# Later first flags of `adj`, far terms a block ahead of the masks, and another order of the last pair's products and rows in a two-layer graph kernel

## The chip, the cores and the metric

The kernel runs on one core of a Trainium2 chip. The metric is device time in microseconds (us), and lower is better. Three runs of the kernel before took 1580.74, 1581.55 and 1582.32 us; the median is 1581.55 us.

The core has five engines that run side by side, each with its own instructions in a fixed order: TensorE (PE in the profile), VectorE (DVE), ScalarE (ACT), GpSimd (POOL) and SyncE (SP). SP and POOL issue nearly all transfers here. The profile's clock of TensorE is given as a share of its full speed.

## The reference

`x` is 4096 x 512, `adj` 4096 x 4096 with some 0.8% of ones. Cut to what matters:

```python
# layer 0
keep = (adj > 0) & (cumsum(adj > 0, axis=1) <= 64)
cnt  = keep.sum(axis=1)
xj = leaky_relu(((keep @ x) / max(cnt, 1)) @ W_nb.T + b_nb)
xi = leaky_relu(x @ W_line.T + b_line)
x  = layernorm(x + xi + where(cnt > 0, xj, 0))
# layer 1
Wh = x @ W + bW
e  = (Wh @ a1 + b1)[:, None] + (Wh @ a2 + b2)[None, :]
e  = where(adj > 0, where(e > 0, e, 0.2 * e), -9e15)
x  = layernorm(x + softmax(e, axis=1) @ Wh)
```

## The kernel before, in words

The rows are 32 blocks of 128. The work runs in four stages, with times from the trace of the profiled execution.

**Linear parts of layer 0 (0 to 218 us).** TensorE computes `x @ W_nb.T` and `x @ W_line.T` first, so that `adj` later multiplies finished rows. After the first two blocks this goes by pairs of blocks, `seven(g, last, codes)` for g = 1 to 13 (the last only ends the pair before): seven products of half-size blocks in place of eight (Strassen's scheme in Winograd's form). Each `product` is two matmuls (four records in the trace, two for each). In the order of TensorE, pair g does: `x_g` with `w11`; the third product of the pair before, `x_p` with `t3`; `bank_z` with `t1`; the pair before's `bank_w` with `w22`; `x_g` with `t2`; the pair before's `x_p` with `t4`; `bank_y` with `w21`. Between them ScalarE copies and bends results, and VectorE transposes the next two blocks of `x` (`turn_pair`, line 325), adds, and forms the low half `y_lo` (line 418) of what ScalarE rounded to `y_hi` (line 417). Line 548 copies `x_g` into `bank_y` and so must wait until line 418 has read the old `bank_y`. `turn_pair` also issues the load of the block three on, `load_turned_x`: four transfers on POOL's queue, line 298.

Into four gaps of each `seven` go steps of another task, the argument `codes`, which finds for each row of `adj` the first 64 ones. Half a row block (2048 columns) at a time is loaded (`load_adj`, SP's queue, line 164), turned into flags by ScalarE (`edge`, line 175), counted by a running sum on VectorE (`scan_sums`, `scan_codes`), packed into bytes by ScalarE (`pack`, line 223) and written out. There are two buffers of each kind, so a load waits for the `edge` two before. At g = 1 the steps are instead `fold_w` (line 386), ten VectorE multiplications that fold `W` with `a1` and `a2`, the small write `wa_d` by SP (line 393), and `edge(0)`. Until the last `fold_w` the rows `a1` and `a2` lie in the buffer that `edge(0)` writes.

**Neighbour sums of layer 0 (218 to 682 us).** Line 741, bound by TensorE; the change doesn't touch it.

**`Wh` of layer 1 (682 to 795 us).** A loop of 32 steps s: four matmuls of block s (line 1045), then VectorE adds the bias for the step before (`finish_wh`, line 818) and transposes the block for step s + 3 (`turn_x1`, line 809). From step 8 on, the weights of the first two blocks of layer 1 are computed beside it. For each quarter block i: `mask` is a ScalarE activation that gives 0 or a huge number, the far term (line 855), and a VectorE subtraction that also takes the row's maximum (line 858); `score` bends the result on ScalarE (line 847). With four quarters done, `greatest` joins the four maxima on VectorE, `shift` bends them (four tiny ScalarE operations, line 847) and forms the negative shift on VectorE (line 891), and `weigh` takes the exponential on ScalarE (line 900), beside the next block's masks.

**Products with the weights (795 us to the end).** 16 pairs of blocks; each sums seven products (`consume`, line 959) over four parts into four PSUM tiles of two halves each, in the order of the table `order`. For the last pair the order is 4, 1, 2, 6, 7, 5, 3, so 4 and 1 share a tile, 2 and 6, 7 and 5, and 3 has its own. The code from line 1109 on ends the last pair. It joins the products into the rows `top` and `low`, scales, adds the residual, normalizes and writes; the `low` row comes first, the `top` row last, in two halves.

The order on each engine is the order of the code (no scheduler moves it); tiles and semaphores only add waits. The lines to follow are these:

```python
601                elif g > 1:
602                    steps = [
603                        lambda: (load_adj(q + 2), edge(q + 1)),
942    order = {True: (1, 2, 4, 7, 5, 6, 3), False: (4, 1, 2, 6, 7, 5, 3)}
```

Of the kernel before, what the change touches and what calls it, by code (L numbers as in the profile page):

```python
# [9 lines left out]
F32 = mybir.dt.float32  # L10
# [22 lines left out]
def two_layer_adj_gnn(  # L33
# [103 lines left out]
    with ExitStack() as l0:  # L137
# [33 lines left out]
        def edge(s):  # L171
            if s < NB * NCH:
                b, h = divmod(s, NCH)
                edge_of[s] = halves_of(adj_p.tile([P, CH], BF16, name="edge"))
                nc.scalar.activation(  # L175
                    edge_of[s], loaded.pop(s).rearrange("p (t q) -> p q t", q=2),
                    AF.Sigmoid, bias=steep[:, 0:1], scale=STEEP,
                    accum_out=cnts[:, h, b : b + 1],
                )
# [103 lines left out]
        with ExitStack() as la:  # L283
# [99 lines left out]
            def fold_w(c):  # L383
                wn = raw["w"][c] if c < NC else early_rows[2]
                for k in range(2):
                    nc.vector.scalar_tensor_tensor(  # L386
                        early_rows[3], wn, 1.0, early_rows[k], ALU.mult, ALU.mult,
                        accum_out=wa[:, k, c : c + 1] if c < NC else ca[:, k : k + 1],
                    )
# [49 lines left out]
            turn_x(1)  # L439
            load_turned_x(4)  # L440

            first = [pls[0]]

# [58 lines left out]
            line(0)  # L502
            bend(0)
            pls[1] = linear(xts.pop(1), "line")
            first.append(pls[1])
            x_top[0] = xt_tile()
            y_low = y_terms(1, pys[1])
            sums_x(1)
# [10 lines left out]

            bank_y, bank_z = pys.pop(0), first[0]
            bank_x, bank_w = [pys.pop(1)], first[1]
            bank_x += [ps_acc.tile([P, C], F32, name="acc") for _ in range(2)]
            low_row, low_line = {}, {}

# [64 lines left out]
            for g in range(1, EDGE // 2):  # L591
                steps = idle
                q = done[0]
                if g == 1:
                    steps = [
                        lambda: (load_adj(1), fold_w(0)),
                        lambda: (fold_w(1), fold_w(2)),
                        idle[0],
                        lambda: (fold_w(3), fold_w(NC), fold_end(), edge(0)),
                    ]  # L600
                elif g > 1:
                    steps = [
                        lambda: (load_adj(q + 2), edge(q + 1)),
                        lambda: scan_sums(q),
                        lambda: pack(q - 1),
                        lambda: scan_codes(q),
                    ]
                    done[0] += 1
                seven(g, False, steps)
# [188 lines left out]
                )  # L798

    x1ts, x1rows, pws, nats, wts, parts = {}, {}, {}, {}, {}, {}  # L800
    m4s, mms, nms, z4s, zqs, rzs, banks, sums = {}, {}, {}, {}, {}, {}, {}, {}

    FIRST = 8

# [41 lines left out]
        bias, scale = st_n[:, i, 0, b : b + 1], st_n[:, i, 2, b : b + 1]  # L846
        nc.scalar.activation(dst, src, AF.Prelu, bias=bias, scale=scale, alpha=0.2)  # L847

    def mask(b, i):

        if i == 0:
            wts[b] = early if b == 0 else wp.tile([P, NI, NS * SQ], F32, name="w")
            m4s[b] = stat.tile([P, NI], F32, name="m4", bufs=2)
        w_i = wts[b][:, i, :]
        nc.scalar.activation(  # L855
            w_i, nats[b, i // 2].bitcast(U8)[:, i % 2, :], AF.Relu, bias=far, scale=-FAR
        )
        nc.vector.tensor_tensor_reduce(  # L858
            w_i, e2_n, w_i, 1.0, -3e38, ALU.subtract, ALU.max, m4s[b][:, i : i + 1]
        )  # L860
        if i % 2:
            load_nat(b + 1, i // 2)

    def score(b, i):
        w_i = wts[b][:, i, :]
        bend1(b, i, w_i, w_i)
# [16 lines left out]
    def shift(b):  # L883


        mm = mms.pop(b)
        lm = stat.tile([P, NI], F32, name="lm", bufs=2)
        for i in range(NI):
            bend1(b, i, lm[:, i : i + 1], mm[:, i : i + 1])
        nms[b] = stat.tile([P, NI], F32, name="nm", bufs=2)  # L890
        nc.vector.scalar_tensor_tensor(  # L891
            nms[b], lm, -1.0, st_n[:, :, 1, b], ALU.mult, ALU.subtract
        )

    def weigh(b, i):
# [43 lines left out]
        }  # L939


    order = {True: (1, 2, 4, 7, 5, 6, 3), False: (4, 1, 2, 6, 7, 5, 3)}
    where = {key: {n: divmod(i, 2) for i, n in enumerate(o)} for key, o in order.items()}

    def consume(q):
# [95 lines left out]
    for s in range(NS):  # L1041
        pws[s] = ps_acc.tile([P, C], F32, name="acc")
        x1t = x1ts.pop(s)
        for m in range(NC):
            nc.tensor.matmul(  # L1045
                pws[s], x1t[:, m, :], ws[:, m, :], start=(m == 0), stop=(m == NC - 1)
            )
        if s > 0:
            finish_wh(s - 1)
        turn_x1(s + 3)  # L1050
        load_turned(s + 7)
        if s == 0:
            load_nat(0, 0)
            load_nat(0, 1)
        if FIRST <= s < FIRST + 8:
            b, i = divmod(s - FIRST, NI)
            mask(b, i)
            score(b, i)
        if FIRST + 4 <= s < FIRST + 12:
            b, i = divmod(s - FIRST - 4, NI)  # L1060
            if i == 0:
                greatest(b)
                shift(b)
            weigh(b, i)
        if s in range(FIRST + 14, FIRST + 22, 2):
            q, part = divmod((s - FIRST - 14) // 2, 2)
            (turn, combine)[part](q)
        elif s >= FIRST + 8:
            combine_wh()
    finish_wh(NS - 1)  # L1070

    for q in range(NP * NT):
        g, k = divmod(q, NP)
        consume(q)
        more = 0 < q < NP * NT - 1
        if more:
            turn(q + 1)

        b = {2: 2 * g + 3, 3: 2 * g + 4}.get(k, 2 if q == 0 else NB)
        if k == 3 and more:  # L1080
            combine(q + 1)
        if b < NB:
            for i in range(NI):
                mask(b, i)
# [26 lines left out]
    x_top, x_low = x1rows[NB - 2].rearrange("p (h c) -> p h c", h=2), x1rows[NB - 1]  # L1111
    stt = nc.vector.scalar_tensor_tensor
    st = stat.tile([P, 2, nc.vector.BN_STATS_DIM], F32, name="st2", bufs=1)
    nc.scalar.copy(top[:, 0], p[1])
    tt(top[:, 1], top[:, 0], p[6], ALU.add)
    tt(top[:, 0], top[:, 0], p[2], ALU.add)
    tt(low[:, 0], top[:, 1], p[7], ALU.add)
    stt(top[:, 0], top[:, 0], rz[:, 0:1], x_top[:, 0], ALU.mult, ALU.add)
    nc.vector.bn_stats(st[:, 0], top[:, 0])
    tt(low[:, 1], low[:, 0], p[5], ALU.add)  # L1120
    tt(low[:, 0], low[:, 0], p[4], ALU.subtract)
    y_low = low.rearrange("p h c -> p (h c)")
    stt(y_low, y_low, rz[:, 1:2], x_low, ALU.mult, ALU.add)
    low_stats = ln_stats(y_low)
    tt(top[:, 1], top[:, 1], p[5], ALU.add)
    stt(top[:, 1], top[:, 1], rz[:, 0:1], x_top[:, 1], ALU.mult, ALU.add)
    stt(top[:, 1], p[3], rz[:, 0:1], top[:, 1], ALU.mult, ALU.add)
    nc.vector.bn_stats(st[:, 1], top[:, 1])
    mv, rs = ln_rs(st)
# [39 lines left out]
```

## Time and profile before

| | |
|---|---|
| median of three runs | 1581.55 us |
| the profiled execution, its own time | 1579.91 us |
| its span in the trace | 1578.1 us |
| mean granted TensorE clock | 0.997 |
| TensorE busy | 1558.7 us (99%) |
| VectorE busy | 1257.6 us (80%) |
| ScalarE busy | 953.7 us (60%) |
| GpSimd busy | 240.6 us (15%) |

The span is the profiled execution from its first to its last instruction. Busy is the time in which an engine has an instruction running. In a timeline each line is a start, a length, the engine, the line of the kernel, the operation, what it writes and reads, and in brackets how long the engine stood idle before it and what ended that. The ends of matmuls are modelled, so distances between starts say more than lengths.

### The profile page before, as it was taken

To read this page: it belongs to the slowest core of one execution; us is meant where nothing else is said; L and a number is where in the kernel's file an instruction comes from. 1 tells how busy PE (TensorE), PEld (TensorE's weight loads), DVE (VectorE), ACT (ScalarE), POOL (GpSimd) and SP (SyncE) were. 2 spreads that over 40 slices of the span, in tenths; PEclk is the share of its full clock that TensorE was granted. 3 is DMA by queue.
4 is the path that set the end of the run, shared out by engine and by line. 5 is a ranking of instruction groups with operands and counts; after the bars stand their busy time and mean duration, and the time that the engine had idled before them with its cause. 6 is when DMAs were issued, how large, how long until landed. Compare 5 with 4: busy or idle time off the path is not lost.

```text
span 1578.1 us, 18600 instructions
## 1 busy us (share of the span) xinstructions
PE 1558.7 (99%) x6408; PEld 1209.3 (77%) x6408; DVE 1257.6 (80%) x2304; ACT 953.7 (60%) x1123; POOL 240.6 (15%) x397
## 2 busy tenths in 40 slices
PE   8999999999999999999999999999999999999997
PEld 4444468888888888854488888888888888888886
DVE  5888658999999998456998888788878878888863
ACT  3666558887888877416165675555765557755520
POOL 4454212222222122120000000000000000000000
PEclk9999999999999999999999999999999999999999
DMA  8756469889889987653211111111111111111100
GB/s 233 200 191 211 159 168 263 261 247 265 238 257 222 275 219 225 154 116 101 58 41 41 28 54 53 42 50 25 48 54 41 54 40 29 54 49 46 41 7 34
DMA packets 170430, 193.01 MB, mean 122 GB/s; under 512 B 101424, under 2 KB 134480, under 8 KB 162144
## 3 DMA queue, kind: packets, MB, share of 16 engines
q1 hardware_dynamic: 147968, 131.38, 30.3%
q0 software_dynamic: 21792, 59.53, 13.0%
q8 instruction: 50, 0.82, 0.2%
q10 hardware_dynamic: 576, 0.92, 0.2%
q14 instruction: 44, 0.36, 0.1%
HBM read 132.91 MB, written 42.08 MB: 111 GB/s over the span
## 4 chain that ended last, share of the span: by engine, by line
PE 95%; DMA 2%; DVE 2%; ACT 1%; issue 1%; SPq 0%; POOL 0%; POOLq 0%; DVEq 0%; ACTq 0%
PE acc L959 35%; PE acc L741 29%; PE pt L959 14%; PE acc L489 8%; PE acc L1045 5%; PE acc L371 2%; DMA a<-in_L_gnn_W_line_dram 1%; DMA c<-in_x_dram 1%; PE pt L371 0%; DMA w<-x_d 0%; DVE edge L386 0%; ACT w L855 0%; DMA own_d<-t 0%; DVE c L809 0%; POOL c L298 0%
## 5 line engine op out<-in xcount | busy, mean ns | idle before, releaser
L959 PE MATMUL acc<-bt,s 128*128 128x256 f32 x1536 | 342.6, 379 | 0.0
L959 PEld LDWEIGHTS acc<-bt,s 128*128 128x128 f32 x1536 | 291.8, 190 | 39.7
L741 PE MATMUL acc<-y_hi,kt 128*128 128x512 f32 x824 | 320.5, 389 | 0.0
L741 PE MATMUL acc<-y_lo,kt 128*128 128x512 f32 x824 | 320.5, 389 | 0.0
L855 ACT ACTIVATE w<-nat,few 128x1024 f32<-128x1024 uint8 x128 | 136.9, 1135 | 289.6 <-DVE a L919 238.9
L959 PE MATMUL acc<-bt,a 128*128 128x256 f32 x1024 | 232.1, 379 | 0.0
L959 PE MATMUL pt<-bt,a 128*128 128x256 f32 x1024 | 231.5, 379 | 0.0
L959 PEld LDWEIGHTS pt<-bt,a 128*128 128x128 f32 x1024 | 194.6, 190 | 26.9 <-issue 0.5
L959 PEld LDWEIGHTS acc<-bt,a 128*128 128x128 f32 x1024 | 194.6, 190 | 26.5
L277 ACT ACTIVATE kt<-ktb,few 128x1024 fp32r<-128x1024 uint8 x124 | 142.7, 1151 | 97.8 <-PE acc L741 80.1
L919 DVE STREAM_TRANSPOSE a<-w 128x1024 f32<-128x1024 f32 x128 | 153.0, 1224 | 57.8 <-ACT w L900 53.2
L126 POOL TENSOR_TENSOR rs<-ve,few 128x1 f32<-128x1 f32 x64 | 46.7, 730 | 945.8 <-DVE ve L124 933.1
L741 PEld LDWEIGHTS acc<-y_hi,kt 128*128 128x128 f32 x824 | 154.7, 188 | 32.2
L741 PEld LDWEIGHTS acc<-y_lo,kt 128*128 128x128 f32 x824 | 154.6, 188 | 32.1
L847 ACT ACTIVATE w<-w,st_n 128x1024 f32<-128x1024 f32 x128 | 149.4, 1233 | 39.0 <-DVE m L858 39.0
L858 DVE CUSTOM_DVE_ANT_0 w<-e_n,w 128x1024 f32<-128x1024 f32 x128 | 149.5, 1220 | 9.1 <-ACT w L855 7.7
L900 ACT ACTIVATE w<-w,nm 128x1024 f32<-128x1024 f32 x128 | 145.4, 1137 | 11.3 <-DVE nm L891 11.3
L175 ACT ACTIVATE edge<-a,few 128x2048 bf16<-128x2048 int32 x64 | 136.2, 2129 | 11.8 <-DVE edge L386 6.8
L223 ACT CAST code<-left 128x2048 uint8<-128x2048 bf16 x64 | 121.1, 1892 | 0.0
L1045 PE MATMUL acc<-w,c 128*128 128x512 f32 x232 | 100.3, 593 | 2.6 <-DVE c L809 2.6
L1045 PEld LDWEIGHTS acc<-w,c 128*128 128x128 f32 x232 | 43.9, 190 | 58.8 <-issue 52.1
L206 DVE TENSOR_TENSOR left<-edge,left 128x2048 bf16<-128x2048 bf16 x64 | 78.4, 1225 | 2.2
(187 smaller groups left out, 1885.3 us busy)
## 6 DMA issues: line engine op xcount, KB each, us to landing
a<-in_adj_dram SPq DMA_DIRECT2D x64, 1024.0 KB, 6.1
code_d<-code POOLq DMA_DIRECT2D x64, 256.0 KB, 4.0
nat<-code_d SPq DMA_DIRECT2D x256, 64.0 KB, 2.0
w<-x_d SPq DMA_DIRECT2D x128, 64.0 KB, 2.1
c<-in_x_dram POOLq DMA_DIRECT2D x124, 64.0 KB, 5.2
own<-in_x_dram SPq DMA_DIRECT2D x31, 256.0 KB, 3.3
own<-own_d POOLq DMA_DIRECT2D x31, 256.0 KB, 5.1
x_d<-own POOLq DMA_DIRECT2D x31, 256.0 KB, 4.7
```

What stands on the lines that cost most here:

```text
L175: nc.scalar.activation(edge_of[s], loaded.pop(s).rearrange("p (t q) -> p q t", q=2), AF.Sigmoid, bias=steep[:, 0:1], scale=STEEP, accum_ou ...
L223: nc.scalar.copy(code.bitcast(U8).rearrange("p (t q) -> p q t", q=2), seen_of.pop(s))
L277: nc.scalar.activation(kts[s], bytes_.rearrange("p t (i r) -> p t r i", r=2), AF.Sigmoid, bias=steep[:, 1:2], scale=STEEP,)
L489: nc.tensor.matmul(bank, lhs[:, k, :], rhs[:, k, :], start=start and k == 0, stop=k == 1, skip_group_check=True,)
L741: nc.tensor.matmul(accs[i], kt[:, k // 2, k % 2, :], term[j], start=(j == 0 and term is y_hi), stop=(j == NB - 1 and term is y_lo),)
L847: nc.scalar.activation(dst, src, AF.Prelu, bias=bias, scale=scale, alpha=0.2)
L855: nc.scalar.activation(w_i, nats[b, i // 2].bitcast(U8)[:, i % 2, :], AF.Relu, bias=far, scale=-FAR)
L858: nc.vector.tensor_tensor_reduce(w_i, e2_n, w_i, 1.0, -3e38, ALU.subtract, ALU.max, m4s[b][:, i : i + 1])
L900: nc.scalar.activation(w_i, w_i, AF.Exp, bias=nms[b][:, i : i + 1], accum_out=z4s[g][:, r, i : i + 1])
L919: nc.vector.transpose(a[:, r].rearrange("p s (i a) -> p i s a", a=SQ), wts[2 * g + r][:, :, ts(k, 8 * SQ)].rearrange("p i (s x) -> p i s x ...
L959: nc.tensor.matmul(banks[g][n], lhs[:, j, :], bt[:, 4 * k + j, rhs, :], start=(k == 0 and j == 0 and n == mate[0]), stop=(k == NP - 1 and ...
L1045: nc.tensor.matmul(pws[s], x1t[:, m, :], ws[:, m, :], start=(m == 0), stop=(m == NC - 1))
```

## The change

It has three parts. First, `edge(0)` moves from the end of pair 1 to the first gap of pair 2, and `edge(1)` from the first gap of pair 2 to its third gap, together with `load_adj(2)`. From pair 3 on the order is as before. Second, `mask` is split into `cover` (the ScalarE activation, and the load of the next bytes of `adj`) and `mask` (the VectorE subtraction); in the `Wh` stage `cover` runs one step ahead of its `mask`. `shift` is split into `bend_greatest` and `less`, and `greatest` moves to the end of the step before, so that two VectorE operations of the loop stand between the maxima and `less`. Third, for the last pair alone, the order of the products becomes 4, 1, 2, 6, 5, 3, 7, so that 5 and 3 share a tile and 7 has its own; the end of the kernel is written anew, with the `top` row whole and first, and the seventh product added to two halves of the `low` row. The name `first` becomes `wide` in one place, which moves nothing.

```diff
-                        lambda: (fold_w(3), fold_w(NC), fold_end(), edge(0)),
+                        lambda: (fold_w(3), fold_w(NC), fold_end()),
                     ]
-                elif g > 1:
+                else:
+                    first = [lambda: edge(0), lambda: (load_adj(q + 2), edge(q + 1))]
                     steps = [
-                        lambda: (load_adj(q + 2), edge(q + 1)),
+                        first[g > 2],
                         lambda: scan_sums(q),
-                        lambda: pack(q - 1),
+                        (lambda: pack(q - 1)) if g > 2 else first[1],
                         lambda: scan_codes(q),
                     ]
...
+    def cover(b, i):
+        if i == 0:
+            wts[b] = early if b == 0 else wp.tile([P, NI, NS * SQ], F32, name="w")
+            m4s[b] = stat.tile([P, NI], F32, name="m4", bufs=2)
+        nc.scalar.activation(
+            wts[b][:, i, :], nats[b, i // 2].bitcast(U8)[:, i % 2, :],
+            AF.Relu, bias=far, scale=-FAR,
+        )
+        if i % 2:
+            load_nat(b + 1, i // 2)
+
     def mask(b, i):
         w_i = wts[b][:, i, :]
-        nc.scalar.activation(
-            w_i, nats[b, i // 2].bitcast(U8)[:, i % 2, :], AF.Relu, bias=far, scale=-FAR
-        )
         nc.vector.tensor_tensor_reduce(
             w_i, e2_n, w_i, 1.0, -3e38, ALU.subtract, ALU.max, m4s[b][:, i : i + 1]
         )
-        if i % 2:
-            load_nat(b + 1, i // 2)
...
-    order = {True: (1, 2, 4, 7, 5, 6, 3), False: (4, 1, 2, 6, 7, 5, 3)}
+    order = {True: (1, 2, 4, 7, 5, 6, 3), False: (4, 1, 2, 6, 5, 3, 7)}
...
-        if FIRST <= s < FIRST + 8:
-            b, i = divmod(s - FIRST, NI)
-            mask(b, i)
-            score(b, i)
-        if FIRST + 4 <= s < FIRST + 12:
-            b, i = divmod(s - FIRST - 4, NI)
-            if i == 0:
-                greatest(b)
-                shift(b)
-            weigh(b, i)
+        k = s - FIRST
+        if k in (4, 8):
+            less(k // NI - 1)
+        if 0 <= k < 8:
+            mask(*divmod(k, NI))
+        if -1 <= k < 7:
+            cover(*divmod(k + 1, NI))
+        if 0 <= k < 8:
+            score(*divmod(k, NI))
+        if k in (3, 7):
+            greatest(k // NI)
+            bend_greatest(k // NI)
+        if 4 <= k < 12:
+            weigh(*divmod(k - 4, NI))
...
+    x_low = x_low.rearrange("p (h c) -> p h c", h=2)
     nc.scalar.copy(top[:, 0], p[1])
+    tt(low[:, 0], top[:, 0], p[4], ALU.subtract)
     tt(top[:, 1], top[:, 0], p[6], ALU.add)
     tt(top[:, 0], top[:, 0], p[2], ALU.add)
-    tt(low[:, 0], top[:, 1], p[7], ALU.add)
+    tt(low[:, 0], low[:, 0], p[6], ALU.add)
+    stt(low[:, 0], low[:, 0], rz[:, 1:2], x_low[:, 0], ALU.mult, ALU.add)
     stt(top[:, 0], top[:, 0], rz[:, 0:1], x_top[:, 0], ALU.mult, ALU.add)
     nc.vector.bn_stats(st[:, 0], top[:, 0])
-    tt(low[:, 1], low[:, 0], p[5], ALU.add)
-    tt(low[:, 0], low[:, 0], p[4], ALU.subtract)
-    y_low = low.rearrange("p h c -> p (h c)")
-    stt(y_low, y_low, rz[:, 1:2], x_low, ALU.mult, ALU.add)
-    low_stats = ln_stats(y_low)
     tt(top[:, 1], top[:, 1], p[5], ALU.add)
+    stt(low[:, 1], top[:, 1], rz[:, 1:2], x_low[:, 1], ALU.mult, ALU.add)
+    tt(top[:, 1], top[:, 1], p[3], ALU.add)
     stt(top[:, 1], top[:, 1], rz[:, 0:1], x_top[:, 1], ALU.mult, ALU.add)
-    stt(top[:, 1], p[3], rz[:, 0:1], top[:, 1], ALU.mult, ALU.add)
     nc.vector.bn_stats(st[:, 1], top[:, 1])
-    mv, rs = ln_rs(st)
-    ln_apply(y_low, low_stats)
-    nc.scalar.dma_start(out_blk(NB - 1), y_low)
+    top_stats = ln_rs(st)
     for h in range(2):
-        ln_apply(top[:, h], (mv, rs))
-        (nc.sync, nc.scalar)[h].dma_start(out_blk(NB - 2)[:, ts(h, HC)], top[:, h])
+        stt(low[:, h], p[7], rz[:, 1:2], low[:, h], ALU.mult, ALU.add)
+    low_stats = ln_stats(low.rearrange("p h c -> p (h c)"))
+    ln_apply(top.rearrange("p h c -> p (h c)"), top_stats)
+    nc.scalar.dma_start(out_blk(NB - 2), top.rearrange("p h c -> p (h c)"))
+    for h in range(2):
+        ln_apply(low[:, h], low_stats)
+        (nc.sync, nc.scalar)[h].dma_start(out_blk(NB - 1)[:, ts(h, HC)], low[:, h])
```

More of the change, by code (lines that the diff above doesn't have):

```diff
@@ L440, in two_layer_adj_gnn @@
             load_turned_x(4)
-            first = [pls[0]]
+            wide = [pls[0]]
             room_hi = last.tile([P, ONE_BY_ONE, C], F32, name="hi")
@@ L504, in two_layer_adj_gnn @@
             pls[1] = linear(xts.pop(1), "line")
-            first.append(pls[1])
+            wide.append(pls[1])
             x_top[0] = xt_tile()
@@ L517, in two_layer_adj_gnn @@
             own(1)
-            bank_y, bank_z = pys.pop(0), first[0]
-            bank_x, bank_w = [pys.pop(1)], first[1]
+            bank_y, bank_z = pys.pop(0), wide[0]
+            bank_x, bank_w = [pys.pop(1)], wide[1]
             bank_x += [ps_acc.tile([P, C], F32, name="acc") for _ in range(2)]
@@ L800, in two_layer_adj_gnn @@
     x1ts, x1rows, pws, nats, wts, parts = {}, {}, {}, {}, {}, {}
-    m4s, mms, nms, z4s, zqs, rzs, banks, sums = {}, {}, {}, {}, {}, {}, {}, {}
+    m4s, mms, lms, nms, z4s, zqs, rzs, banks, sums = ({} for _ in range(9))
     FIRST = 8
@@ L847, in bend1 @@
         nc.scalar.activation(dst, src, AF.Prelu, bias=bias, scale=scale, alpha=0.2)
-    def mask(b, i):
+    def cover(b, i):
         if i == 0:
@@ L853, in mask @@
             m4s[b] = stat.tile([P, NI], F32, name="m4", bufs=2)
+        nc.scalar.activation(
[4 more added lines that the diff above has]
+            load_nat(b + 1, i // 2)
+    def mask(b, i):
         w_i = wts[b][:, i, :]
-        nc.scalar.activation(
-            w_i, nats[b, i // 2].bitcast(U8)[:, i % 2, :], AF.Relu, bias=far, scale=-FAR
-        )
         nc.vector.tensor_tensor_reduce(
@@ L883, in shift, with bend_greatest, less @@
     def shift(b):
+        bend_greatest(b)
+        less(b)
+    def bend_greatest(b):
         mm = mms.pop(b)
-        lm = stat.tile([P, NI], F32, name="lm", bufs=2)
+        lms[b] = stat.tile([P, NI], F32, name="lm", bufs=2)
         for i in range(NI):
-            bend1(b, i, lm[:, i : i + 1], mm[:, i : i + 1])
+            bend1(b, i, lms[b][:, i : i + 1], mm[:, i : i + 1])
+    def less(b):
         nms[b] = stat.tile([P, NI], F32, name="nm", bufs=2)
         nc.vector.scalar_tensor_tensor(
-            nms[b], lm, -1.0, st_n[:, :, 1, b], ALU.mult, ALU.subtract
+            nms[b], lms.pop(b), -1.0, st_n[:, :, 1, b], ALU.mult, ALU.subtract
         )
@@ L1083, in two_layer_adj_gnn @@
             for i in range(NI):
+                cover(b, i)
                 mask(b, i)
```

## The prediction

> **What bounds the kernel now.** I read the page's head first, then the timeline of TensorE for holes, then at each hole the timelines of ScalarE and VectorE, the granted clock by stretch, and the transfers.
>
> ```profile
> span 1578.1 us, 18600 instructions
> PE 1558.7 (99%) x6408; PEld 1209.3 (77%) x6408; DVE 1257.6 (80%) x2304; ACT 953.7 (60%) x1123; POOL 240.6 (15%) x397
> ```
>
> TensorE bounds it. Only its holes and the tail after its last matmul can be won. Up to 42 us the waits on TensorE are for first loads that the change doesn't touch. After it the timeline has three holes (start, length, work, and the idle time ahead of it with what ended it):
>
> ```profile
> 39.99 1.88 PE L489 MATMUL acc<-wt_line,lo 128*128 128x512 f32 x4
> 44.49 2.54 PE L489 MATMUL acc<-hi,lo 128*128 128x512 f32 x4 [2.62 <-ACT acc L548]
> 46.82 3.07 PE L489 MATMUL acc<-hi,xt 128*128 128x512 f32 x4
> 49.73 3.60 PE L489 MATMUL acc<-wt_nb,xt 128*128 128x512 f32 x8
> ...
> 747.94 3.70 PE L1045 MATMUL acc<-w,c 128*128 128x512 f32 x8 [0.35 <-DVE c L809]
> 753.87 41.47 PE L1045 MATMUL acc<-w,c 128*128 128x512 f32 x96 [2.23 <-DVE c L809]
> ```
>
> The first has an aftermath, by stretch (time, then each engine's busy time, then the clock):
>
> ```profile
> 44.49:46.90 2.41, 2.41 (x5) 1.09 (x6) 2.38 (x4) 2.41 (x3) 2.21 (x5) 0.77 0.12 24
> 46.90:49.70 2.80, 2.80 (x5) 1.12 (x4) 2.77 (x5) 1.82 (x4) 2.12 (x4) 0.59 0.41 29
> ```
>
> Four records take 1.72 us elsewhere (from 38.27 to 39.99), here 2.33 and 2.91: 1.80 us lost besides. So this hole costs 2.78 (44.49 - 41.71) and 1.80. On ScalarE, `edge(0)` holds the queue up to 40.37, and behind it stand y_hi and L548; at 742 each of its steps waits 1.30 us:
>
> ```profile
> 32.28 1.28 ACT L175 ACT_TABLE_LOAD   x1
> 40.37 2.13 ACT L175 ACTIVATE edge<-a,few 128x2048 bf16<-128x2048 int32 x1 [6.80 <-DVE edge L386]
> 741.99 1.24 ACT L847 ACTIVATE w<-w,st_n 128x1024 f32<-128x1024 f32 x1 [1.30 <-DVE m L858]
> ```
>
> VectorE waits for ScalarE in turn (43.09, 745.43), once for a block of x (58.14), is late with L809 at 753.11, for which TensorE stands still, and owns the tail:
>
> ```profile
> 43.09 0.69 DVE L418 TENSOR_TENSOR y_lo<-acc,y_hi 128x512 fp32r<-128x512 f32 x1 [2.56 <-ACT y_hi L417]
> 58.14 0.71 DVE L325 STREAM_TRANSPOSE xt<-c 128x512 f32<-128x512 f32 x1 [3.73 <-DMA c<-in_x_dram]
> 745.43 1.23 DVE L858 CUSTOM_DVE_ANT_0 w<-e_n,w 128x1024 f32<-128x1024 f32 x1 [2.26 <-ACT w L855]
> 753.11 0.70 DVE L809 STREAM_TRANSPOSE c<-w 128x512 f32<-128x512 f32 x1
> 1567.19 0.42 DVE L1117 TENSOR_TENSOR c<-c,acc 128x256 f32<-128x256 f32 x1 [2.52 <-PE acc L959]
> 1574.39 0.73 DVE L131 TENSOR_SCALAR c<-c,mv,rs 128x256 f32<-128x256 f32 x2 [0.44 <-POOL rs L126]
> ```
>
> The transfers near the first hole land late (last column, us), for hardly any bytes move from 42 to 50 us:
>
> ```profile
> wa_d<-wa SPq DMA_DIRECT2D x1, 4.0 KB, 12.6
> a<-in_adj_dram SPq DMA_DIRECT2D x1, 1024.0 KB, 12.6
> c<-in_x_dram POOLq DMA_DIRECT2D x3, 64.0 KB, 11.1
> ```
>
> **What the Trainium skill says.** "TensorE: Matmul & The Clock Gate", Part 1, gives half clock after an idle window of about 3.4 us, the windows running free. Here records stand 0.85 us apart rather than 0.43 from 45.97 to about 49.3, one such window; the hole at 751 has none, so 2.5 us of idleness may or may not cost it. The same part calls ScalarE and VectorE strict first-in first-out: the 6.80 us wait with y_hi behind it agrees. "DMA: Bandwidth & Descriptors", Queues, rings and completion order, has each engine alternate between queues packet by packet; no view here shows the alternation.
>
> **Part 1, flags later.** ScalarE now meets y_hi first (its product, first half of the eight records at 32.58, ends at 34.3), and y_hi is ready long before VectorE wants it. VectorE ends the folds at 40.45, then L418 to 41.1; L548 runs 41.2 to 41.8. TensorE, free at 41.71, starts at 41.8, not 44.49: 2.7. Nothing of the clock is lost then: 1.8 more, 4.5 in all. What moves behind: the table load (1.28) loses its idle cover and stands before `edge(0)`, which runs 43.0 (41.7 + 1.28) to 45.2. `scan_sums(0)` starts at 45.3 (before 45.48), so VectorE gains nothing here. Its L574 follows 4.1 later, to 49.4; TensorE wants that at 48.7 (41.8 + 4 products of 1.72), a loss of 0.7. L548 of pair 3 ends at 54.3 for a product wanted at 54.6. So `x_p` with `t4` could start at 56.3 where it now starts at 60.03: 3.7.
>
> It also needs L556, which stands behind the transposes of blocks 8 and 9. Block 9 landed at 58.0. Its four POOL issues follow L325 of block 6, now at 41.1 rather than 43.7, so they go 2.6 us earlier; POOL has nothing ahead of them. Load 2 of `adj` goes the other way: it waits for `edge(0)`, so 45.2 rather than 42.6, and load 3 for `edge(1)`, 49.6 rather than 46.6. `wa_d` stays at 38.9 and, if it is what holds the transfers, clogs them up to its landing at 51.5. If the clog alone decides, block 9 still lands at 58 and part 1 keeps 0.6; if its issue does, at 55.4, it keeps 3.2. I take 56, nearer to the issue, because block 9 is then in its queue ahead of load 2 rather than behind it: L325 and L556 (1.4) give 57.4, so **2.6**. Load 2 then has to land by 57.3: `edge(2)`, lines 558 to 565 and L574 take 5.2, and TensorE wants that at 62.5. Landed at 55.2 before; I estimate 56 to 57: by 52 us only 0.4 MB of it had moved, and the rest shares some 300 GB/s (0.75 MB in the 2 us from 52) with block 9. From pair 5 on VectorE waits for TensorE (L574 at 84.33 and after), so the lead is kept; the same holds at 218, where the first packed weights end at 216.4 and follow the last y_hi.
>
> **Part 2, far terms ahead.** In blocks 0 and 1 a ScalarE step was 4.71 us (737.28 to 741.99), 1.30 of it the wait; L855 ahead of it leaves 3.41 against TensorE's 3.43. VectorE per step: 0.63 + 1.15 + 0.6 = 2.4, without the 2.26. From step 8 on (713.1) I get L858 always 2.0 us after the end of its TensorE step, apart from step 12, 2.9. The table load of L900 (1.28) puts ScalarE 1.3 behind; it catches up, since L858 needs `cover` only by then. `less` of block 1 comes at 1.9 after the end of step 16, the ready bend being 1.85, with L818 and L809 ahead of it; L809 has two steps of slack. SP's `load_nat` moves one step ahead too and waits for a `cover` that ends at most 0.6 after a step, ahead of the next L809 at 0.85, so it holds up no block load. Both holes go: 0.35, and 753.87 - 747.94 - 8 x 0.429 = 2.50. **2.8**, bounded by 0 below (the wait on ScalarE comes back under another name) and by 2.8 plus a half-clock window of 1.8 above, where a run has one. Cover gone: if `cover` were late by more than two steps the hole would return. From q = 0 on the orders on ScalarE and VectorE don't change.
>
> **Part 3, the end.** L1117 wanted product 7 but shares a tile with 5, so it ran at 1567.19, and 14 VectorE operations followed. Now the tile of 5 and 3 is full at that same moment (sixth product), and before it the left half of both rows is done: 1563.80 + 6 operations (0.42 to 0.52 apart) = 1566.5. Then by starts: L1139 1567.19, +0.45, +0.5, +0.45, +0.52 statistics 1569.1, +0.46, +0.24, +0.1 gives L1146 at 1569.9. Product 7 ended at 1568.9, so no wait. Two halves 0.9, statistics 0.73, 0.21, then POOL's power as before (1573.34 to 1574.39: 1.05): the last two L131 at 1572.9 rather than 1574.39. `top` and its issue on ScalarE's queue fit in that wait. **1.5**. Product 7 last keeps the transposed weights until its `consume` ends, which leaves VectorE 12 us for 5 us of work: nothing.
>
> **Sum.** 2.6 + 2.8 + 1.5 = 6.9 us. The profiled execution took 1579.91, its span 1578.1. So 1573.0 there, a span of 1571.2; the median lies 1.64 above it: **1574.6**.
>
> **Rivals.** (a) The transfers take most of part 1: 0.6 + 2.8 + 1.5 = 4.9, 1576.7. For: the clog. Against: block 9 is issued earlier and `adj` later. (b) All three, and no clog: 3.7 + 2.8 + 1.5 and the 1.64, if the medians lie higher for half clock after the second hole as well: 9.6, 1571.9. (c) Part 2 doesn't do it, since ScalarE at 3.41 of 3.43 has no slack, and (a) too: 2.1, 1579.5, not to be told from no change. (d) Slower, one mechanism: load 2 of `adj`, issued 2.6 later behind block 9 and 10, becomes the wait. Each us after 57.3 is lost; at 59.9 part 1 gives nothing, and with a half-clock window (1.8) anew it outweighs the other 4.3 from about 62.4 on, 17 us after its issue. At 64 it would be 1583. The longest `adj` transfer there took 14.6.
>
> **How the numbers follow.** Forecast 0.60, own range 1573 to 1576; (a) 0.17; (b) 0.10; (c) 0.09; (d) 0.04. 0.2% is 3.2 us, about what a measurement of this kernel can tell from no change: faster below 1578.4. So faster 0.87, same 0.09, slower 0.04. The range 1572.2 to 1578.2 leaves out (d), most of (c) and part of (b).
>
> **What would show it.** TensorE: no hole at 42 us, clock 1.00 to 50 us, a hole of about 1 us near 56, behind L325 and L556; none from 682 to 795, that stage 2.8 shorter; ScalarE's L847 without the 1.30. At the end L131 some 4 us after TensorE's last matmul, now 5.5. Wrong if block 9 lands at 58, `edge(2)` waits for `adj` past 57.3, or new holes halve the clock.

## The result, and the profile after

The changed kernel takes 1572.71 us (median of four runs, 1571.71 to 1573.83); the kernel before, run beside it, 1581.24 us (four runs, 1580.74 to 1582.32). The ratio is 0.9945, with a 95% interval of 0.9928 to 0.9963. The forecast was 1574.6 us, with a range of 1572.2 to 1578.2. The profiled execution took 1573.12 us, its span 1571.3; worked out beforehand were 1573.0 and 1571.2.

The head of the page of the changed kernel:

```profile
span 1571.3 us, 18597 instructions
PE 1558.7 (99%) x6408; PEld 1210.7 (77%) x6408; DVE 1258.6 (80%) x2306; ACT 952.7 (61%) x1123; POOL 239.2 (15%) x397
```

That TensorE is busy for the same 1558.7 us as before is chance. From its first L489 to `x_p` with `t3` of pair 4, where the half clock was, it is busy for 33.83 us rather than 35.10; ahead of that first L489, where the change moves nothing, for 24.14 us rather than 22.45. So 1.3 us of the gain lie within its instructions, and the rest between them and after the last. The timeline of TensorE around the place of the first old hole:

```profile
40.76 1.88 PE L489 MATMUL acc<-wt_line,lo 128*128 128x512 f32 x4
42.62 1.98 PE L489 MATMUL acc<-hi,lo 128*128 128x512 f32 x4
44.44 1.88 PE L489 MATMUL acc<-hi,xt 128*128 128x512 f32 x4
46.15 3.60 PE L489 MATMUL acc<-wt_nb,xt 128*128 128x512 f32 x8
50.34 1.98 PE L489 MATMUL acc<-wt_line,lo 128*128 128x512 f32 x4 [0.59 <-DVE acc L574]
...
62.95 1.98 PE L489 MATMUL acc<-wt_line,lo 128*128 128x512 f32 x4 [0.33 <-DVE acc L574]
```

The wait of 2.62 us is gone, and the products follow each other at 1.7 to 1.9 us. Two smaller waits have appeared, both on L574. By stretch (time, busy time of TensorE, weight loads, VectorE, ScalarE and GpSimd, the granted clock, the DMA share, GB/s) the clock is now full where it was 0.77 and 0.59:

```profile
44.00:46.00 2.00, 2.00 (x6) 0.95 (x5) 0.00 (x0) 2.00 (x2) 2.00 (x4) 1.00 2.89 33
48.00:50.00 2.00, 1.75 (x5) 0.44 (x3) 1.97 (x4) 2.00 (x2) 0.00 (x0) 1.00 0.52 27
```

Where the two new waits come from is read on ScalarE, first, and then on VectorE:

```profile
41.99 0.57 ACT L548 COPY acc<-acc 128x512 f32<-128x512 f32 x1 [6.14 <-DVE y_lo L418]
42.58 1.28 ACT L175 ACT_TABLE_LOAD   x1
43.87 2.14 ACT L175 ACTIVATE edge<-a,few 128x2048 bf16<-128x2048 int32 x1
...
57.78 2.16 ACT L175 ACTIVATE edge<-a,few 128x2048 bf16<-128x2048 int32 x1 [2.65 <-DMA a<-in_adj_dram]
```

```profile
54.39 1.29 DVE L325 STREAM_TRANSPOSE xt<-c 128x512 f32<-128x512 f32 x2
...
62.20 0.70 DVE L574 TENSOR_TENSOR acc<-t,acc 128x512 f32<-128x512 f32 x1 [2.44 <-ACT t L565]
```

The table load stands between L548 and `edge(0)` with nothing to hide it, and delays the scan behind it; that is the wait at 50.34. The second wait is another matter. Both transposes at 54.39 run one behind the other without a wait: block 9 of `x` had landed. `edge(2)` waited 2.65 us for load 2 of `adj`, and L574 stood behind `edge(2)`. The load of `adj` issued between 46 and 48 us, with the time to landing in the last column:

```profile
a<-in_adj_dram SPq DMA_DIRECT2D x1, 1024.0 KB, 11.6
```

The second old stretch of holes, in the `Wh` stage of layer 1, and the start of the next stage, on TensorE; then two `score` steps on ScalarE:

```profile
680.08 10.46 PE L1056 MATMUL acc<-w 128*128 128x512 f32 x24
690.38 99.73 PE L1056 MATMUL acc<-w,c 128*128 128x512 f32 x232
789.95 3.62 PE L970 MATMUL pt<-bt,a 128*128 128x256 f32 x16
```

```profile
723.35 1.24 ACT L848 ACTIVATE w<-w,st_n 128x1024 f32<-128x1024 f32 x1 [1.15 <-DVE m L865]
...
732.36 1.23 ACT L848 ACTIVATE w<-w,st_n 128x1024 f32<-128x1024 f32 x1
```

All 232 matmuls are one unbroken stretch. ScalarE still waits for the masks of block 0, when it has nothing else to do; from 732 us on the 1.30 us per step are gone. At the end, VectorE, and TensorE's last group:

```profile
1561.96 0.42 DVE L1139 TENSOR_TENSOR c<-c,acc 128x256 f32<-128x256 f32 x1 [0.87 <-PE acc L970]
1564.69 0.87 DVE L1146 SCALAR_TENSOR_TENSOR c<-acc,rz,c 128x256 f32<-128x256 f32 x2
1567.59 0.73 DVE L131 TENSOR_SCALAR c<-c,mv,rs 128x256 f32<-128x256 f32 x2 [0.44 <-POOL rs L126]
```

```profile
1561.76 1.89 PE L970 MATMUL acc<-bt,a 128*128 128x256 f32 x8
```

TensorE ends at about 1563.6, and the last L131 starts 3.9 us later; before it was 5.5. L1146, which takes in the seventh product, does not wait for it.

The balance of the two profiled executions, part by part:

| stretch | before | after | gain |
|---|---|---|---|
| first L489 starts (first loads) | 26.95 | 27.71 | -0.76 |
| from there to `x_p` with `t3` of pair 4 | 38.22 | 35.24 | 2.98 |
| from there to the `Wh` stage of layer 1 | 617.03 | 617.13 | -0.10 |
| `Wh` stage of layer 1 | 112.98 | 109.87 | 3.11 |
| from there to the end of the span | 782.92 | 781.35 | 1.57 |
| sum | 1578.1 | 1571.3 | 6.8 |

The first row is no effect of the change: in the profiled executions of this case that start varies from 26.78 to 28.9 us, whatever the kernel.

### The profile page after: what moved, and what is told of

Same layout as the page of the kernel before. It is cut to its first block, busy times and chain, and to the rows that moved or that the text cites. A ratio compares the mean times of both kernels' runs of the same rounds, so it can differ in the third digit from the quotient of the medians.

```text
span 1571.3 us, 18597 instructions
## 1 busy us (share of the span) xinstructions
PE 1558.7 (99%) x6408; PEld 1210.7 (77%) x6408; DVE 1258.6 (80%) x2306; ACT 952.7 (61%) x1123; POOL 239.2 (15%) x397
## 4 chain that ended last, share of the span: by engine, by line
PE 96%; DMA 1%; DVE 1%; ACT 0%; issue 0%; POOLq 0%; POOL 0%; DVEq 0%; ACTq 0%
PE acc L970 35%; PE acc L742 30%; PE pt L970 14%; PE acc L489 7%; PE acc L1056 7%; PE acc L371 3%; DMA a<-in_adj_dram 1%; PE pt L371 0%; DMA c<-in_x_dram 0%; PE pt L153 0%; DVE edge L386 0%; DMA xb<-in_x_dram 0%; ACT edge L175 0%; ACT wt_line L154 0%; PE acc L357 0%
```

## The experiments

### One part alone, and the clock

The prediction's sum takes the three parts as independent. So each was put into the kernel before alone; and a fourth kernel asks whether the half clock after the first hole comes from the hole.

Part 1 alone, in the kernel before:

```diff
-                        lambda: (fold_w(3), fold_w(NC), fold_end(), edge(0)),
+                        lambda: (fold_w(3), fold_w(NC), fold_end()),
...
+                    first = [lambda: edge(0), lambda: (load_adj(q + 2), edge(q + 1))]
```

> The kernel before with part 1 alone (the flags of adj later). Theory, the three parts add up and part 1 is worth what the trace after shows: TensorE starts the product with t2 of pair 2 about 2.6 us earlier and at full clock, and keeps about 3.0 us up to 218 us; time 1578.2 us against 1581.2, ratio 0.998. Rival, part 1 keeps nothing by itself because load 2 of adj eats it: 1581, ratio 1.000.

Measured: 1580.27 us (13 runs), against 1581.32 (49 runs) of the kernel before beside it; ratio 0.9994 (0.9986 to 1.0003). That is 1.05 us, where the prediction's sum has 2.6 for this part. Yet at its own place the part did its work: `x_p` with `t3` of pair 4 starts at 63.54, in an execution that began 0.99 us later than that of before, so 2.6 us are won there. They are given back 690 us later. TensorE at the hole of the `Wh` stage, and the clock by stretch after it:

```profile
752.35 43.16 PE L1046 MATMUL acc<-w,c 128*128 128x512 f32 x96 [2.23 <-DVE c L810]
```

```profile
752.35:754.35 2.00, 2.00 (x3) 0.97 (x4) 1.93 (x5) 1.81 (x4) 0.00 (x0) 0.61 0.26 76
754.35:756.35 2.00, 2.00 (x4) 0.73 (x3) 1.93 (x6) 0.00 (x0) 0.00 (x0) 0.54 0.28 79
```

The same 96 matmuls took 41.47 us before, behind a hole of the same 2.23 us. Here the clock drops after the hole: read in steps of 0.5 us, it is at 0.50 from about 752.8 to 756.2 us, a stretch of 3.4 us, and 1.69 us are lost. Both the theory and its rival were wrong as stated: neither had the loss there.

Part 2 alone, with `cover`, `bend_greatest` and `less` and the new order in the loop:

```diff
+        if k in (4, 8):
+            less(k // NI - 1)
+        if 0 <= k < 8:
+            mask(*divmod(k, NI))
+        if -1 <= k < 7:
+            cover(*divmod(k + 1, NI))
```

> The kernel before with part 2 alone (far terms a step ahead, maxima and shift split). Theory: the Wh stage takes 109.9 us from its first to its last matmul's end, not 113.0; time 1578.1 us, ratio 0.998. Rival, in plain executions the second hole also costs half a clock window that the profiled execution of before did not show: 1576.4 us, ratio 0.997.

Measured: 1577.81 us (13 runs), ratio 0.9981 (0.9973 to 0.9989), so 3.5 us. In its trace the stage takes 109.86 us, as in the changed kernel, and has no hole. The time lies between the theory and the rival, nearer to the theory.

Part 3 alone, the new order of the last pair with the new end:

```diff
-    order = {True: (1, 2, 4, 7, 5, 6, 3), False: (4, 1, 2, 6, 7, 5, 3)}
+    order = {True: (1, 2, 4, 7, 5, 6, 3), False: (4, 1, 2, 6, 5, 3, 7)}
```

> The kernel before with part 3 alone (order of the last pair's products and the new end). Theory: the last two L131 start 4.0 us after TensorE's last matmul, not 5.5; time 1579.7 us, ratio 0.999, and nothing else moves. Rival, product 7 last holds back the transposes of the last pair: holes of TensorE after 1510 us, no gain, 1581.

Measured: 1579.85 us (21 runs), ratio 0.9987 (0.998 to 0.9993), so 1.5 us between the medians, as predicted. But the runs fall into two groups: 13 have a mean clock of 0.997 and a median of 1580.22 us, eight have 0.999 and 1577.64. So the median mixes part 3 with what the clock took, and the agreement is partly luck. What shows part 3 is the trace: L131 starts 3.9 us after TensorE's last matmul, as in the changed kernel, and the rival's holes ahead of it do not come.

The first hole filled: five matmuls of 256 columns into a spare tile, read by nobody, ahead of the product that waits for L548 in pair 2 of the kernel before.

```diff
+                    if g == 2:
+                        fill(5)
                     product(x_g, s2, t2)
```

> The kernel before with five matmuls of 256 columns added on TensorE ahead of the product with t2 of pair 2, into an idle PSUM tile; nothing reads them. They fill some 2.15 of the 2.6 us of the first hole. Theory, the 0.77 and 0.59 of clock after that hole come from the idleness: the product still starts at 44.5, its records stand 0.43 apart, clock 1.00 from 44.5 to 50, 1.8 us gained in the trace, 1579.4 us, ratio 0.999. Rival, the slow records have another cause (the engines and transfers at work beside them): the same 0.85 apart, 1581 us.

Measured: 1580.74 us (13 runs), ratio 0.9996 (0.9988 to 1.0004). The clock did what the theory says; the time did not follow. By stretch, over the same two stretches that the prediction shows of the kernel before, and then on TensorE's timeline:

```profile
44.49:46.90 2.41, 1.94 (x8) 1.18 (x7) 2.17 (x4) 1.60 (x3) 0.57 (x2) 1.00 1.57 27
46.90:49.70 2.80, 2.80 (x8) 1.17 (x7) 2.77 (x3) 2.77 (x5) 2.80 (x6) 1.00 0.32 38
```

```profile
61.02 1.98 PE L489 MATMUL acc<-hi,lo 128*128 128x512 f32 x4 [0.89 <-DVE lo L562]
```

The clock is 1.00 where it was 0.77 and 0.59, so it was the idleness that halved it. But of the 1.7 us won by 50 us only 0.5 are left at `x_p` with `t3` of pair 4: TensorE runs into a new wait of 0.89 us for L562, the sum behind the transpose of block 9, which lands as late as it did. This is the limit that the prediction feared for the changed kernel. It is real here, where `turn_pair` stands at its old place; the change moves it forward.

### Does the clock explain what part 1 gave back?

Part 1 as above, and four such matmuls in the hole of the `Wh` stage, before step 20.

```diff
+        if s == 20:
+            ...
+            for _ in range(4):
+                nc.tensor.matmul(pt[:, : C // 2], ws[:, 0, :P], ws[:, 0, : C // 2], start=True, stop=True)
```

> The kernel before with part 1 alone, as in the run of part 1, and four matmuls of 256 columns added on TensorE ahead of step 20 of the Wh stage; nothing reads them. They fill some 1.7 of the 2.2 us of the second hole. Theory, part 1 alone gave little because its executions lost a half-clock window after the second hole: with the hole filled the clock stays 1.00 there, the stage takes 113.0 us, not 114.7, and the time is 1578.6 us, not 1580.3, ratio 0.9983. Rival, the clock after that hole has another cause: 1580.3 us as for part 1 alone.

Measured: 1578.27 us (18 runs; the kernel before beside it 1581.34, 23 runs), ratio 0.9981 (0.9974 to 0.9988). The kernel with part 1 alone, on another chip, took 1580.27 against nearly the same 1581.32, so the four extra matmuls, whose result nobody reads, win some 2 us. TensorE's timeline and the clock behind the hole:

```profile
750.16 1.89 PE L1046 MATMUL pt<-w 128*128 128x256 f32 x8
752.55 41.47 PE L1050 MATMUL acc<-w,c 128*128 128x512 f32 x96 [0.51 <-DVE c L810]
```

```profile
752.55:754.55 2.00, 2.00 (x5) 1.04 (x6) 1.93 (x5) 1.81 (x4) 0.00 (x0) 1.00 0.26 76
```

The stage stands still for as long as before, but the clock stays full and the 96 matmuls take 41.47 us again. So a half-clock stretch is what took part 1's gain, and part 1 is worth about 3 us once that is out of the way.

### What limits the changed kernel at 50 and 62 us?

Three kernels, and the changed kernel again, on one chip one after the other. The changed kernel took 1573.91 us (five runs, 1573.09 to 1574.02), ratio 0.9954 (0.9942 to 0.9967), against 1581.1 for the kernel before (nine runs).

> The changed kernel itself, measured beside the others in more runs. Theory, with no hole left no execution loses a clock window, so the gain is the 6.8 us of the profiled execution and, over many runs, about 1 us more, since executions of before lose one window or two: some 7.5 us, ratio 0.9953. Rival, the three parts are worth in plain runs only what they are worth alone (1.0 + 3.5 + 1.5 = 6.0 us): ratio 0.9962.

The interval takes in both the theory's 0.9953 and the rival's 0.9962, so these runs alone do not decide between them.

The small write `wa_d` moved from pair 1 behind the last pair:

```diff
             def fold_end():
                 nc.vector.tensor_tensor(ca, ca, b12, ALU.add)
+
+            def write_wa():
                 nc.sync.dma_start(wa_d.rearrange("k (c p) -> p k c", p=P), wa)
...
+            write_wa()
             y_last = [last.tile([P, ONE_BY_ONE, C], F32R
```

> The changed kernel with the small write of wa_d (4 KB) issued after the last pair of the first stage, not in pair 1. Theory, that write holds up the transfers from 42 to 51 us: load 2 of adj lands some 6 to 7 us after its issue, not 11.6, and the hole of 0.33 us at pair 4 goes, the one of 0.59 at pair 3 stays; 0.3 us gained, not to be told in the time. Rival, the transfers are slow there for another reason: 11.6 us again and the same holes.

Measured: 1573.46 us (1572.73 to 1573.91), ratio 0.9952 (0.9938 to 0.9965), not to be told from the changed kernel by time. The trace tells them apart. The same load of `adj` as above, ScalarE's `edge(2)`, and what is left on TensorE:

```profile
a<-in_adj_dram SPq DMA_DIRECT2D x1, 1024.0 KB, 5.6
```

```profile
55.52 0.57 ACT L550 COPY acc<-acc 128x512 f32<-128x512 f32 x1 [3.23 <-DVE y_lo L420]
56.00 2.20 ACT L175 ACTIVATE edge<-a,few 128x2048 bf16<-128x2048 int32 x1
```

```profile
51.30 1.98 PE L491 MATMUL acc<-wt_line,lo 128*128 128x512 f32 x4 [0.59 <-DVE acc L576]
```

Without the 4 KB write a load of 1 MB takes 5.6 us rather than 11.6, `edge(2)` does not wait, and the hole at 62 us is gone. The blocks of `x` land in 2.2 us rather than 9, and those issued beside the load of `adj` in 4.0 to 5.5 rather than 11. The write now goes out at 150.9 us, and the slow transfers go with it. Those issued from 150 to 158 us, first in the changed kernel, then with the write there:

```profile
a<-in_adj_dram SPq DMA_DIRECT2D x1, 1024.0 KB, 5.8
own_d<-t POOLq DMA_DIRECT2D x2, 256.0 KB, 3.6
code_d<-code POOLq DMA_DIRECT2D x1, 256.0 KB, 2.7
```

```profile
a<-in_adj_dram SPq DMA_DIRECT2D x1, 1024.0 KB, 10.3
own_d<-t POOLq DMA_DIRECT2D x2, 256.0 KB, 12.6
code_d<-code POOLq DMA_DIRECT2D x1, 256.0 KB, 12.2
wa_d<-wa SPq DMA_DIRECT2D x1, 4.0 KB, 14.7
```

There TensorE has no wait for them. So the clog is `wa_d`: it goes where the write is taken away and comes where it is put. The wait of 0.59 us behind the table load stays, as it should.

The table load moved under idle time instead: a one-column sigmoid, whose result nobody reads, in front of the last folds of pair 1.

```diff
+            def early_table():
+                nc.scalar.activation(spare_one, three, AF.Sigmoid, bias=steep[:, 0:1], scale=STEEP)
...
-                        lambda: (fold_w(3), fold_w(NC), fold_end()),
+                        lambda: (early_table(), fold_w(3), fold_w(NC), fold_end()),
```

> The changed kernel with one added ScalarE activation of a single column in pair 1, ahead of y_hi, so that its table is loaded in ScalarE's idle time at 33 us. Theory, the table load is what holds edge(0): it starts 1.3 us earlier, scan_sums(0) and load 2 of adj with it, both holes (0.59 and 0.33) go; 0.9 us gained on the changed kernel, ratio 0.9947 where the changed kernel has 0.9953. Rival, VectorE is the bound there: edge(0) is earlier and the holes stay.

Measured: 1571.89 us (1570.56 to 1572.81), ratio 0.9943 (0.993 to 0.9955). On ScalarE:

```profile
34.20 1.28 ACT L397 ACT_TABLE_LOAD   x1
...
43.62 2.16 ACT L176 ACTIVATE edge<-a,few 128x2048 bf16<-128x2048 int32 x1
...
57.10 2.15 ACT L176 ACTIVATE edge<-a,few 128x2048 bf16<-128x2048 int32 x1 [2.20 <-DMA a<-in_adj_dram]
```

`edge(0)` follows the copy of L552 at once, and TensorE has no hole from 38.4 us up to the `Wh` stage's end. The load of `adj` still takes 11.2 us, but, counted from the first L489, it is issued 1.4 us earlier, and the wait for it no longer reaches TensorE.

Both together:

> The changed kernel with the early table and the late write of wa_d. Theory: no hole of TensorE from 42 us to the end of the products, load 2 of adj out of the way, the best of these kernels by 0.9 us or a little more; ratio 0.9946. Rival, the late write now holds up the transfers at 175 to 190 us and costs a hole there.

Measured: 1571.89 us (1570.77 to 1572.68), ratio 0.9943 (0.993 to 0.9955); its profiled execution has a span of 1569.0 us, in part because it started early (first L489 at 26.78). The rival's hole at 175 to 190 us does not come. All ten runs of these two kernels lie below all five of the changed kernel beside them, by 2.0 us in the medians, where 0.9 had been expected. From the wait of 0.2 us at about 29 us to the `Wh` stage, the changed kernel takes 650.27 us, these two 648.82 and 648.83. Of the 1.45 us between, 0.92 are the two holes; the rest I have not traced. With the table load out of the way, moving `wa_d` adds nothing more. So on this chip the version with the early table load, one instruction of 0.29 us more, is better than the kernel before and the changed kernel, by a small amount.

### Which half of parts 2 and 3 does it?

`cover` a step ahead as in the change, but maxima, bends and `less` joined again in front of `weigh`, as before:

```diff
-        if k in (4, 8):
-            less(k // NI - 1)
...
-        if k in (3, 7):
-            greatest(k // NI)
-            bend_greatest(k // NI)
         if 4 <= k < 12:
-            weigh(*divmod(k - 4, NI))
+            b, i = divmod(k - 4, NI)
+            if i == 0:
+                greatest(b)
+                shift(b)
+            weigh(b, i)
```

> The changed kernel with the maxima and the shift of the first two blocks joined again at the place they had before; cover stays a step ahead. Theory, it is the waits of L858 on ScalarE (2.26 us in each of three steps) that put VectorE behind, so this alone takes away the second hole: 1572.7 us as the changed kernel. Rival, the 1.3 us for the bend and the order of the maxima are needed too: a hole of about 1 us at step 20, 1573.7 us or more.

Measured: 1573.54 us (five runs), ratio 0.9952 (0.994 to 0.9965), and on TensorE the whole stretch of 232 matmuls without a hole:

```profile
690.36 99.73 PE L1056 MATMUL acc<-w,c 128*128 128x512 f32 x232
```

The cover ahead is enough. The stage takes 109.86 us.

The converse, the maxima a step earlier and `less` split off, but `cover` right in front of its `mask`:

```diff
         if 0 <= k < 8:
+            cover(*divmod(k, NI))
             mask(*divmod(k, NI))
-        if -1 <= k < 7:
-            cover(*divmod(k + 1, NI))
```

> The changed kernel with cover in the same step as its mask, as before; only the maxima and the shift are split. Theory: L858 waits 2.2 us in each step of the second block again and L809 of step 17 comes about 1.5 us earlier than before, so a hole of about 1 us is left; 1573.7 us. Rival, the maxima alone take the hole away: 1572.7 us.

Measured: 1576.55 us (six runs), ratio 0.997 (0.9959 to 0.9982), 3.0 us slower than the kernel above, beside which it ran. TensorE, and VectorE ahead of it:

```profile
748.63 44.90 PE L1056 MATMUL acc<-w,c 128*128 128x512 f32 x104 [2.12 <-DVE c L810]
```

```profile
744.34 1.23 DVE L865 CUSTOM_DVE_ANT_0 w<-e_n,w 128x1024 f32<-128x1024 f32 x1 [2.26 <-ACT w L855]
```

The stage takes 112.25 us, 0.73 less than in the kernel before; the small hole is gone, but the large one is nearly as long as it was, where I had expected about half of it to go. The mask waits its 2.26 us for ScalarE, and the nine small operations of `greatest` then stand in front of L819 and L810, so that the block that TensorE needs is late. The early maxima alone do little. The time missed both the theory and the rival: of the 3.0 us to the kernel above, the stage explains 2.4; the rest is not traced.

For the last pair, the new end with the old order of products:

```diff
-    order = {True: (1, 2, 4, 7, 5, 6, 3), False: (4, 1, 2, 6, 5, 3, 7)}
+    order = {True: (1, 2, 4, 7, 5, 6, 3), False: (4, 1, 2, 6, 7, 5, 3)}
```

> The changed kernel with its new end, but the last pair's products in the old order 4, 1, 2, 6, 7, 5, 3. Theory, the right half of the top row then waits for product 3, the last: its addition at the end of TensorE's work and not 1.7 us before it, so the last L131 come 4.7 us after TensorE's last matmul, not 4.0; 1573.4 us. Rival, the new end gives the whole 1.5 us and the order nothing: 1572.7 us.

Measured: 1574.75 us (five runs), ratio 0.9958 (0.9944 to 0.9971). On VectorE:

```profile
1564.37 0.42 DVE L1141 TENSOR_TENSOR c<-c,acc 128x256 f32<-128x256 f32 x1 [0.79 <-PE acc L970]
...
1569.01 0.73 DVE L131 TENSOR_SCALAR c<-c,mv,rs 128x256 f32<-128x256 f32 x2 [0.44 <-POOL rs L126]
```

L1141 now waits for product 3, which is the last one again, and the rest of the end stands behind it. The last L131 starts 4.7 us after the last matmul, so that of the 1.5 us some 0.7 come with the order and 0.8 with the new end. (The new order with the old end was not run.) The changed kernel did not run beside this one, and the times alone do not separate the two.

## Why the prediction was right, and where it was not

**Part 1, the first hole and its clock: right.** L548 no longer stands behind `edge(0)`; the product starts at 42.62, right behind L548 and with no wait that the timeline lists, and the clock is full up to 50 us. The table load in front of `edge(0)` and the wait for L574 in pair 3 came as worked out: 0.7 expected, 0.59 measured. One small reading was off: of the waits of TensorE up to 42 us in the kernel before, those at 29.04 and 36.45 (0.22 and 0.28 us) are for ScalarE and VectorE, not for first loads; the change leaves them.

**Part 1, the step with the transfers: the wrong one of two.** The step said that block 9 of `x`, landing at 56 us, would hold up L556 and leave 2.6 us, and that load 2 of `adj` would be in time. It was the other way round. Block 9 was issued 2.6 us earlier, as said, but its transfers, issued from 42.8 us on, took 9.1 us in the median, and the transpose had it at 54.39 without a wait. Load 2 was late. The bound of 57.3 is in the time of the kernel before; in the changed kernel's trace TensorE was free for the product at 62.62, which puts the bound 5.2 us earlier, at 57.4, and `edge(2)` began at 57.78. So rival (d) was the mechanism, at a cost of 0.33 us. The hole of about 1 us near 56 us that the prediction named as a sign did not come. Its working also took 0.75 MB in 2 us as some 300 GB/s; it is 375.

That part 1 nevertheless brought about what was forecast is luck of two sizes close to each other. The size also varies: up to the start of `x_p` with `t3` of pair 4, the seven traces that have part 1 with the table load and `wa_d` at their places gain from 2.4 to 3.4 us, with a wait there of 0.95 us at most and in two of them none. The changed kernel's 2.98 is one draw of this, and the 2.6 that was worked out lies inside it. Rival (a), the clog holding block 9 until 58 us, is refuted in the changed kernel, but the first filled hole shows that block as the limit in the old order.

**The clog itself: right, and now shown.** The prediction named `wa_d` as what holds the transfers, if anything does; moving it halves the time of the load, and slows the transfers at its new place.

**Part 2: right, with one term too small.** Worked out were 2.8 us, measured 3.11. By the starts of the matmuls the second hole was 2.50, as worked out, but the first was 0.50, where the sum took the 0.35 of listed idle time; the last 0.11 lie in the 96 matmuls behind the second hole. The claim that ScalarE at 3.41 of 3.43 us per step keeps up is borne out, so rival (c) is out. What the prediction lists as three measures, cover ahead, maxima early and `less` apart, is one: the experiments put all of it on the cover.

**Part 3: right.** 1.5 worked out, 1.57 measured; some 4 us after the last matmul, measured 3.9. L1146 took in product 7 without a wait, as said.

**Adding the parts: right for the profiled execution, not for the median.** The trace gains 3.0 + 3.1 + 1.6 - 0.1, less 0.8 for the late start, 6.8 in all where 6.9 was worked out. That this is so close is luck again: without the late start the parts gain 7.6. The median came out 1.9 us below the forecast. The step that failed there is the last one, which set the median 1.64 us above the profiled execution, as in the kernel before; in the changed kernel it lies 0.41 us below. (The second comparison, with 1573.91, is 0.7 below the forecast.)

What bears on that step in the experiments is the half clock. In plain runs the parts alone win 1.05, 3.5 and 1.5, together 6.0, and all three together 8.5 in one comparison and 7.2 in the other. With the second hole filled, part 1 wins 3.1 rather than 1.05, which would make the sum 8.1. The profiled execution of before has one half-clock stretch, after the first hole. Its runs differ: 16 of 49 have a mean clock of 0.996 and a median of 1582.47 us, the other 33 have 0.997 or 0.998 and 1581.03. The kernel with part 1 alone has one stretch too, after the second hole, and 0.997 in all 13 runs; eight runs with part 3 alone have 0.999, with both holes in place. The changed kernel has no hole over 0.6 us left after 30 us, and its runs have 0.998 or 0.999. So rival (b)'s reason for a larger gain, half clock after the second hole as well, is probably part of why the median came out low; its other half, no clog, was wrong. How many stretches each plain run has cannot be seen, since only the profiled ones have a trace.

The Trainium skill, "TensorE: Matmul & The Clock Gate", Part 1, speaks of free-running windows of about 3.4 us and of one idle window that halves the clock. On the windows the traces agree: in the four that have a half-clock stretch after a hole it lasts 3.4 us, and it begins 0.4 us after the product has started in two of them and 1.3 us after in the other two. But the holes that brought it are of 2.2 to 2.6 us, shorter than a window, and the same hole of 2.23 us brought it in one kernel's trace and not in another's. A hole that lies in one window may count where one that is cut by the edge between two does not; no run here tests that.

## What to carry to other kernels

Price a hole on TensorE by its length plus a half-clock stretch (here 1.7 us lost) that may or may not follow, and judge an edit by the trace at its own place before its total: closing one hole of two can show as nothing until the other is closed too. When a step is moved on an in-order queue, move what it drags along, such as a table load, into idle time by a small instruction of the same kind further ahead. After moving a consumer forward, list every transfer that it needs and its landing time, and ask what slows those transfers down; here it was a write of 4 KB.

## What the runs showed of the hardware

- **A small write in very many packets slows the transfers beside it.** `wa_d` has 4 KB. In the changed kernel its queue shows 1040 packets with 0.00 MB from 30 to 46 us, when it carries nothing else, and the write lands 12.0 us after its issue. While it is under way a 1 MB load takes 11.6 us instead of 5.6 and a 64 KB load 9 instead of 2.2. Issued at 150.9 us instead, it slows the transfers there in the same way (10.3 instead of 5.8, 12.2 instead of 2.7).
- **A hole of 2.2 to 2.6 us can halve the clock.** Holes of 2.23 (part 1 alone) and 2.62 us (before, part 2 alone, part 3 alone) were followed by 3.4 us at 0.50; holes of 0.5 us, left by filler matmuls, were not. Nor were holes of 2.23 us in the kernel before and with part 3 alone.
- **A table load costs 1.28 us and nothing more here.** The Trainium skill, "ScalarE: Activation LUTs", What ACT_TABLE_LOAD costs, adds about 1.38 us of drain to it. In the changed kernel the load starts at 42.58 and `edge(0)` at 43.87, so 1.29 us in all; the trace has no such drain.
